# A rotary swap by one VectorE shuffle, and mask, scale and row maximum of attention scores in one VectorE operation per head and query tile

## The chip, the cores and the metric

The kernel runs on one core of a Trainium2 chip. The metric is the device time of one execution in microseconds (us), the median of several runs. The core's engines work side by side, each through an in-order queue of its own: TensorE (PE) multiplies matrices into PSUM, VectorE (DVE) and ScalarE (ACT) compute on PSUM and SBUF, GpSimd (POOL) computes on SBUF, and SyncE (SP) issues most transfers. They wait for one another by semaphores.

## The reference, cut to what matters

The input x is 4 x 512 x 1024 in fp32. It is layer-normalized; an attention with rotary embedding (16 heads of 64) and a gate (a linear layer with the signs of its weights, scaled by routed expert scales, then SiLU) are computed from it, and the result is x + attention * gate.

```python
def _rotate_every_two(x):
    r = jnp.stack((x[..., 1::2], x[..., ::2]), axis=-1)
    return r.reshape(x.shape)

def _apply_rotary(x, sin, cos):
    sin = jnp.repeat(sin[None, :, None, :], 2, axis=3)
    cos = jnp.repeat(cos[None, :, None, :], 2, axis=3)
    return x * cos + _rotate_every_two(x) * sin
...
q = jnp.concatenate([_apply_rotary(q[..., :ROT], sin, cos), q[..., ROT:]], axis=-1)
k = jnp.concatenate([_apply_rotary(k[..., :ROT], sin, cos), k[..., ROT:]], axis=-1)
...
logits = jnp.einsum('bhqd,bhkd->bhqk', q, k)
causal = jnp.tril(jnp.ones((s, s), dtype=bool))[None, None]
logits = jnp.where(causal, logits, MASK_VAL)
logits = logits / jnp.sqrt(jnp.float32(HEAD_DIM))
attn = jax.nn.softmax(logits, axis=-1)
out = jnp.einsum('bhqk,bhkd->bhqd', attn, v)
...
xn = _layernorm(x, axis=-1)
s = _L0_attn_ref(xn, L0_attn_Wq, L0_attn_Wk, L0_attn_Wv, L0_attn_Wo)
g = _silu(_L0_ffn_ref(xn, L0_ffn_weight, L0_ffn_bias, ...))
x = x + s * g
```

Two things of it matter here. The rotary embedding pairs each even column of a head with the odd column beside it: it needs, next to q and k themselves, a copy in which neighbours have changed places. And the scores are masked causally, scaled by 1/8 and put through a softmax over the keys.

## The kernel before

*Stages.* The work falls into an attention stage (to about 780 us of the profiled execution), a short stage in which the last attention units run beside the gate's first products, and an output stage of Strassen products for the gate and the output projection (from about 825 us). PE's instructions have an order written out by hand: the kernel's Python code emits them in the order in which PE runs them. DVE, ACT, POOL and SP are ordered by the scheduler, except where the code pins an instruction, and during the first 27 us for DVE and ACT.

*Attention.* For each of the 4 batches and each of 4 groups of head pairs, Q, K and (for two groups at once) V are projected by seven Strassen products each (`project_qk`, `project_v`). Between the matmuls of these projections, the attention of the group before is interleaved in pieces: a group has two units, each a pair of heads (two times 64 partitions). That makes 32 units. One unit goes through:

1. `rotary` (L313), once for Q and once for K, each a tile `c` of 128 partitions (2 heads x 64) by 512 positions. The host has reordered the columns of Wq and Wk so that the 32 even columns of a head come first and its 32 odd columns after them. The swapped copy `sw` is thus four block copies of 32 partitions (L319, L320 on ACT), with the factor 1/8 for Q. DVE multiplies `c` with the cosines (L321), POOL multiplies `sw` with the sines and adds (L322, L323).
2. `scores` (L508): for the query tiles 3, 2, 0, 1 (128 queries each, against 512, 384, 128 and 256 keys) two heads each, into PSUM. Tiles 3, 2 and 0 use the pool `ps_sc`; tile 1 uses two banks of the ring of four (`bank`), which the projections use too.
3. `softmax` (L533), first for tiles 1 and 3 and in a later piece for 2 and 0: DVE adds the mask to the diagonal 128 columns (L545), and takes the negated row maximum (L548), for both heads at once except in tile 1; ACT computes the exponential with that bias and sums it (L551, each followed by a read of its accumulator); DVE inverts the sum (L559), POOL multiplies (L561).
4. `transpose_blocks` (L569): DVE transposes blocks of 32 x 32 (L579), and sixteen transfers on SP's queue set them into place (L589).
5. `values` (L596): the products with V into one ring bank (L604), which ACT copies out (L613); then a transfer to DRAM.

The ring of four PSUM banks is what ties the engines together: a projection's product, the two score banks of tile 1, the p·V bank and the transposes of x all take their turn in it, and PE can start on a bank only when ACT or DVE has emptied it. In the projections, ACT copies out parts (L358, L387), DVE adds them (L352, L389) and forms the Strassen sums of the next weights (`form_w`, L288).

*Around it.* The next batch's x is normalized (L171 to L187), transposed by PE (L200) and copied from PSUM to `X`, on DVE where the test of L203 holds (13 copies, L204) and else on ACT (19 copies, L206). The router of a batch (`router`) uses `gw` and writes a transposed result `rT` (L671).

Of the kernel before, what the change touches and what calls it, by code (L numbers as in the profile page):

```python
# [9 lines left out]
F32 = mybir.dt.float32  # L10
F32R = mybir.dt.float32r
AF = mybir.ActivationFunctionType
ALU = mybir.AluOpType
AX = mybir.AxisListType
# [6 lines left out]
B, S, E = 4, 512, 1024  # L21
H, D = 16, 64
NE = 8
P = 128
NT = B * S
NC = E // P
NPAIR = H // 2
NGRP = NPAIR // 2
TPB = S // P
# [2 lines left out]
MASK_VAL = -1000000000.0  # L32
EPS = 1e-05
SCALE = 0.125

QCOL = [0, P, 3 * P, 6 * P]
OFF = [0, 128, 256, 224]


@with_exitstack
def attn_gated_ffn_kernel(
# [15 lines left out]
    nc = tc.nc  # L59
# [3 lines left out]
    cp = ctx.enter_context(tc.tile_pool(name="const", bufs=1))  # L63
    st = ctx.enter_context(tc.tile_pool(name="stats", bufs=4))
# [2 lines left out]

    ident = cp.tile([P, P], F32, name="ident")
    make_identity(nc, ident)
    mask = cp.tile([P, P], F32, name="mask")  # L70
    nc.gpsimd.memset(mask, 0.0)
    nc.gpsimd.affine_select(
        out=mask,
        in_=mask,
        compare_op=ALU.is_ge,
        fill=MASK_VAL,
        base=0,
# [6 lines left out]
    warm = cp.tile([P, 1], F32, name="warm")  # L84
    nc.scalar.activation(warm, eps, AF.Sqrt)

    gw = cp.tile([P, NC, 32], F32, name="gw")
    nc.gpsimd.memset(gw, 0.0)

# [5 lines left out]
    for sign, base in ((1, 0), (-1, 7)):  # L97
        nc.gpsimd.affine_select(
            out=high,
            in_=high,  # L100
# [29 lines left out]
    def left(*a, **k):  # L130
        return pctx.enter_context(tc.tile_pool(*a, **k))
# [6 lines left out]
    wp = left(name="w", bufs=3)  # L138
    tmp = left(name="tmp", bufs=2)
    tabs = left(name="tables", bufs=1)  # L140

    cos_sb = tabs.tile([P, S], F32, name="cos_sb")
    sin_sb = tabs.tile([P, S], F32, name="sin_sb")

    def bank(name):
        return ring.tile([P, S], F32, tag="r", name=name)

    def tp_bank(name):
        return bank(name).rearrange("p (t q) -> p t q", t=TPB)
# [44 lines left out]
    def transpose_x(b, t, g):  # L194
        if b not in X:
            X[b] = xp.tile([P, NC, S], F32, tag="X", name=f"X_{b}")
        tp = tp_bank(f"xtp_{b}_{t}_{g}")
        for j in range(4):
            c = 4 * g + j
            nc.tensor.transpose(tp[:, j, :], xin[b, t][:, c * P : (c + 1) * P], ident)  # L200
        dst = X[b][:, 4 * g : 4 * g + 4, t * P : (t + 1) * P]

        if (g == 0 and b > 0) or (g == 1 and (b, t) == (0, TPB - 1)):  # L203
            nc.vector.tensor_copy(dst, tp)  # L204
        else:
            nc.scalar.copy(dst, tp)  # L206
        if g == 1:

            queue = nc.scalar if (b, t) == (B - 1, TPB - 1) else nc.sync
            queue.dma_start(  # L210
                out=xn_d[b, t].rearrange("p (c q) -> p c q", c=NC),
                in_=X[b][:, :, t * P : (t + 1) * P],
            )
# [98 lines left out]

    def rotary(u, m, c):  # L313

        sc = SCALE if m == 0 else 1.0
        rot = qk.tile([P, S], F32, tag=f"rot{m}", name="rot%d_%d_%d_%d" % (m, *u))
        sw = tmp.tile([P, S], F32, tag="sw", name="sw%d_%d_%d_%d" % (m, *u))
        for r in range(0, P, 64):
            nc.scalar.activation(sw[r : r + 32, :], c[r + 32 : r + 64, :], AF.Copy, scale=sc)  # L319
            nc.scalar.activation(sw[r + 32 : r + 64, :], c[r : r + 32, :], AF.Copy, scale=sc)  # L320
        nc.vector.scalar_tensor_tensor(rot, c, sc, cos_sb, op0=ALU.mult, op1=ALU.mult)  # L321
        nc.gpsimd.tensor_tensor(sw, sw, sin_sb, op=ALU.mult)  # L322
        nc.gpsimd.tensor_tensor(rot, rot, sw, op=ALU.add)  # L323
        (Q, K)[m][u] = rot
# [177 lines left out]
    def probs(u, i):  # L502

        return PR[u][:, :, QCOL[i] : QCOL[i] + (i + 1) * P]
# [28 lines left out]
    def softmax(u, *tiles):  # L533
        un = "%d_%d_%d" % u
        for i in tiles:
            pt, ps = probs(u, i), SC[u, i]
            nmx = st.tile([P, 2], F32, tag="nmx", name=f"nmx_{un}_{i}")

            at_once = [(ps[h][:, None, :], slice(h, h + 1)) for h in range(2)]
            if i != 1:  # L540
                at_once = [(ps, slice(0, 2))]
                ps = [ps[:, h, :] for h in range(2)]
            for v, hs in at_once:
                diag = v[:, :, i * P : (i + 1) * P]
                nc.vector.tensor_tensor(  # L545
                    diag, diag, mask[:, None, :].to_broadcast((P, hs.stop - hs.start, P)), op=ALU.add
                )
                nc.vector.tensor_reduce(nmx[:, hs], v, AX.X, ALU.max, negate=True)  # L548
            ssum = st.tile([P, 2], F32, tag="ssum", name=f"ssum_{un}_{i}")
            for h in range(2):  # L550
                nc.scalar.activation(  # L551
                    pt[:, h, :],
                    ps[h],
                    AF.Exp,
                    bias=nmx[:, h : h + 1],
                    accum_out=ssum[:, h : h + 1],
                )
            rs = st.tile([P, 2], F32, tag="rs", name=f"rs_{un}_{i}")
            nc.vector.reciprocal(rs, ssum)  # L559
            for h in range(2):  # L560
                nc.gpsimd.tensor_scalar(  # L561
                    pt[:, h, :], pt[:, h, :], rs[:, h : h + 1], 1.0,
                    op0=ALU.mult, op1=ALU.mult,
                )
# [4 lines left out]
    def transpose_blocks(u, queues=(nc.sync,), ordered=False):  # L569
# [4 lines left out]
        for j in range(TPB):  # L574
            for i in range(j, TPB):
                src = probs(u, i)[:, :, j * P : (j + 1) * P]
                o = OFF[j] + 32 * (i - j)
                tc.keep_in_program_order(
# [17 lines left out]
    def values(u):  # L596
# [3 lines left out]
        for j in range(TPB):  # L600
            for h in range(2):
                r = h * D
                o = 320 * h + OFF[j]
                nc.tensor.matmul(  # L604
# [19 lines left out]
    def router(b, step):  # L624
        if step == 0:
            lg = bank(f"lg_{b}")[:, :P]
            for c in range(NC):
                for t in range(TPB):
                    nc.tensor.matmul(
                        lg[32 * t : 32 * t + 32, :],  # L630
                        lhsT=gw[:, c, :],
                        rhs=X[b][:, c, t * P : (t + 1) * P],
                        start=(c == 0),
                        stop=(c == NC - 1),
                    )
            R["lg"] = st.tile([P, P], F32, tag="r", name=f"lgs_{b}", bufs=1)
            nc.scalar.copy(R["lg"], lg)
        elif step == 1:
            lt = bank(f"lt_{b}")[:, :P]
            nc.tensor.transpose(lt, R["lg"], ident)  # L640
            ltg = lt.rearrange("p (t e) -> p t e", e=32)[:, :, :NE]
            nmx = st.tile([P, TPB], F32, tag="rmx", name=f"rmx_{b}")
            nc.vector.tensor_reduce(nmx, ltg, AX.X, ALU.max)
            ex = st.tile([P, TPB, 32], F32, tag="r", name=f"rex_{b}", bufs=1)
            exv = ex[:, :, :NE]
            nc.vector.tensor_tensor(
                exv, ltg, nmx[:, :, None].to_broadcast((P, TPB, NE)), op=ALU.subtract
            )
            nc.scalar.activation(exv, exv, AF.Exp)
            ssum = st.tile([P, TPB], F32, tag="rsum", name=f"rsum_{b}")  # L650
            nc.vector.tensor_reduce(ssum, exv, AX.X, ALU.add)
            rs = st.tile([P, TPB], F32, tag="rrs", name=f"rrs_{b}")
            nc.vector.reciprocal(rs, ssum)
            nc.vector.tensor_tensor(
                exv, exv, rs[:, :, None].to_broadcast((P, TPB, NE)), op=ALU.mult
            )

            hi = st.tile([P, TPB, NE], F32R, tag="rhi", name=f"rhi_{b}", bufs=1)
            nc.vector.tensor_copy(hi, exv)
            hi = hi.bitcast(F32)  # L660
            for n in (3, 2):
                nc.vector.tensor_tensor(
                    ex[:, :, n * NE : (n + 1) * NE], exv, hi, op=ALU.subtract
                )
            for n in (1, 0):
                nc.vector.tensor_copy(ex[:, :, n * NE : (n + 1) * NE], hi)
            R["ex"] = ex
        else:
            rt = bank(f"rt_{b}")[:, :P]
            nc.tensor.transpose(rt, R["ex"].rearrange("p t e -> p (t e)"), ident)  # L670
            rT = st.tile([P, P], F32, tag="rT", name=f"rT_{b}", bufs=1)  # L671
            nc.vector.tensor_copy(rT, rt)
            for t in range(TPB):
                nc.sync.dma_start(out=rt_d[b, t], in_=rT[32 * t : 32 * t + 32, :])
# [215 lines left out]
    for k, (b, g) in enumerate(groups):  # L890
# [38 lines left out]
        if k in (5, 9, 12, 14):  # L929
            n = {5: 0, 9: 2, 12: 4, 14: 6}[k]  # L930
# [121 lines left out]
    w, v = late  # L1052
# [318 lines left out]
def _rotary_tables():  # L1371
    f = np.float32
    inv = (f(1.0) / (f(10000.0) ** (np.arange(0, D, 2, dtype=f) / f(D)))).astype(f)
    ang = (np.arange(S, dtype=f)[None, :] * inv[:, None]).astype(f)
    return np.tile(np.cos(ang), (4, 1)).astype(f), np.tile(np.sin(ang), (4, 1)).astype(f)


# [49 lines left out]
```

## Time and profile before

| | |
|---|---|
| runs | 1107.7, 1110.0, 1110.54 us, median 1110.0 |
| span of the profiled execution | 1108.7 us |
| granted clock of PE, mean | 0.996 |
| ACT swaps, L319 and L320 | 256 times 628 ns, 160.7 us |
| DVE mask, L545 | 160 times, 57.0 us busy |
| DVE row maximum, L548 | 160 times, 105.2 us busy |
| ACT exponentials, L551 | 256 times, 132.9 us busy |
| POOL rotary products, L322 and L323 | 128 times, 175.9 us busy |

How to read the lines: a row of a group names the line of the kernel, the engine, the operation, the tiles (out<-in) and shapes, how often it ran, then busy time in us and the mean of one in ns, and last the idle time of that engine just before these instructions and who ended most of it. A row of the waits says which engine and line waited for which, in total us, how often, and the longest. A timeline row begins with the start and the length in us; what stands in brackets is the idle time before it. PE runs each fp32 matmul in two passes, so that "x16" stands for eight matmuls of the code. A row of stretches gives the bounds, the length, and the busy time of PE, the weight loads, DVE, ACT and POOL (with their number of instructions), then the granted clock, the share of the transfers and GB/s. The mean of one instruction contains the overlap with its neighbour; the busy time counts overlaps once.

### The profile page before, as it was taken

The numbers are of one execution on the slowest core, as the hardware profiler recorded it, in microseconds if no ns is written. First come the engines' busy times: TensorE is split into PE (matmuls) and PEld (weight loads), VectorE is DVE, ScalarE is ACT, GpSimd is POOL, SyncE is SP. The second block draws the span as 40 slices with busy tenths as digits, with TensorE's granted clock in tenths as the row PEclk, the third lists the DMA queues.
The fourth block names the chain that finished last, engine by engine and source line by source line (L and its number), as shares of the span: only waits on it lengthen the run. The fifth ranks groups of instructions, "written<-read, shape, count | busy, mean of one in ns | idle before, by whom it ended". The sixth has DMA issues, their size and how long they took to land. (4 is left out here: it accounts for less than half of the span.)

```text
span 1108.7 us, 15895 instructions
## 1 busy us (share of the span) xinstructions
PE 1087.4 (98%) x5176; PEld 790.2 (71%) x5176; DVE 870.4 (79%) x1740; ACT 461.3 (42%) x1072; POOL 518.9 (47%) x566
## 2 busy tenths in 40 slices
PE   9999999999999999999999999999999999999997
PEld 8887778777777877777788687777664545654663
DVE  7888888788988978888887887887776877567663
ACT  2452754453375445427544452655530223122220
POOL 0772645555264555526453562675552433432334
PEclk9999999999999999999999999999999999999999
DMA  9415566544556654455666445544664222431331
GB/s 323 135 69 147 149 184 189 160 137 119 166 155 187 190 154 135 121 163 158 184 183 219 140 148 142 153 125 122 179 193 171 90 93 102 148 119 54 136 114 57
DMA packets 86770, 163.88 MB, mean 148 GB/s; under 512 B 13472, under 2 KB 49056, under 8 KB 80672
## 3 DMA queue, kind: packets, MB, share of 16 engines
q1 hardware_dynamic: 80144, 152.25, 46.1%
q0 software_dynamic: 4832, 9.05, 2.4%
q10 hardware_dynamic: 1712, 1.57, 0.5%
q8 instruction: 41, 0.67, 0.3%
q14 instruction: 41, 0.34, 0.1%
HBM read 95.45 MB, written 25.43 MB: 109 GB/s over the span
## 5 line engine op out<-in xcount | busy, mean ns | idle before, releaser
L561 POOL TENSOR_SCALAR p<-p,rs 128x256 f32<-128x256 f32 (+3 forms) x256 | 183.7, 734 | 200.6 <-DVE rs L559 136.2
L551 ACT ACTIVATE p<-sc,nmx 128x256 f32<-128x256 f32 (+3 forms) x256 | 132.9, 529 | 104.8 <-DVE nmx L548 87.2
L338 PE MATMUL pj<-X,w 128*128 128x256 f32 x576 | 134.3, 382 | 1.7 <-ACT p L551 1.5
L338 PE MATMUL pj<-T,S 128*128 128x256 f32 x512 | 120.5, 385 | 8.5 <-ACT v L613 8.5
L579 DVE STREAM_TRANSPOSE y<-p 128x256 f32<-128x256 f32 x320 | 112.4, 409 | 18.3 <-POOL p L561 16.9
L322 POOL TENSOR_TENSOR sw<-sw,sin_sb 128x512 f32<-128x512 f32 x64 | 85.1, 1330 | 81.1 <-ACT sw L320 75.4
L338 PEld LDWEIGHTS pj<-X,w 128*128 128x128 f32 x576 | 108.1, 190 | 20.0 <-issue 2.9
L338 PEld LDWEIGHTS pj<-T,S 128*128 128x128 f32 x512 | 96.7, 192 | 24.8 <-ACT v L613 11.3
L319 ACT ACTIVATE sw<-c 32x512 f32<-32x512 f32 x128 | 80.3, 628 | 70.0 <-DVE c L352 68.2
L338 PE MATMUL pj<-T,w 128*128 128x256 f32 x448 | 106.6, 382 | 0.0
L548 DVE TENSOR_REDUCE nmx<-sc 128x1 f32<-128x256 f32 (+3 forms) x160 | 105.2, 683 | 1.3
L425 PE MATMUL pj<-w,X 128*128 128x256 f32 x416 | 94.6, 380 | 0.8 <-ACT p L551 0.5
L338 PEld LDWEIGHTS pj<-T,w 128*128 128x128 f32 x448 | 83.4, 190 | 15.5 <-issue 4.6
L323 POOL TENSOR_TENSOR rot<-rot,sw 128x512 f32<-128x512 f32 x64 | 90.8, 1419 | 5.0
L425 PEld LDWEIGHTS pj<-w,X 128*128 128x128 f32 x416 | 78.2, 190 | 12.7 <-ACT p L551 2.0
L545 DVE TENSOR_TENSOR sc<-sc,mask 128x256 f32<-128x256 f32 (+1 forms) x160 | 57.0, 371 | 35.3 <-PE sc L525 35.3
L320 ACT ACTIVATE sw<-c 32x512 f32<-32x512 f32 x128 | 80.4, 628 | 1.6
L425 PE MATMUL pj<-w,T 128*128 128x256 f32 x352 | 80.2, 381 | 0.0
L525 PE MATMUL sc<-rot,rot 64*128 64x128 f32 (+3 forms) x512 | 79.7, 443 | 0.3 <-DVE v L451 0.3
L604 PE MATMUL pv<-p,v 128*64 128x256 f32 (+3 forms) x512 | 76.0, 439 | 0.4 <-issue 0.4
L388 POOL TENSOR_TENSOR part<-part,part 128x256 f32<-128x256 f32 x32 | 24.7, 771 | 105.2 <-ACT part L387 102.0
L613 ACT COPY v<-pv 128x512 f32<-128x512 f32 x32 | 18.7, 585 | 131.5 <-PE pv L604 131.4
(177 smaller groups left out, 1956.9 us busy)
## 6 DMA issues: line engine op xcount, KB each, us to landing
p<-y SPq DMA_DIRECT2D x496, 80.0 KB, 2.1
w<-in_wqk SPq DMA_DIRECT2D x31, 1024.0 KB, 5.3
w<-in_wv SPq DMA_DIRECT2D x16, 1024.0 KB, 5.2
x<-in_x SPq DMA_DIRECT2D x16, 512.0 KB, 4.3
at_d<-v SPq DMA_DIRECT2D x32, 256.0 KB, 2.7
xp<-xn_d SPq DMA_DIRECT2D x16, 512.0 KB, 4.6
ap<-at_d SPq DMA_DIRECT2D x16, 512.0 KB, 5.1
xr<-in_x SPq DMA_DIRECT2D x32, 256.0 KB, 3.0
```

Source lines behind the costliest of these rows:

```text
L319: nc.scalar.activation(sw[r : r + 32, :], c[r + 32 : r + 64, :], AF.Copy, scale=sc)
L320: nc.scalar.activation(sw[r + 32 : r + 64, :], c[r : r + 32, :], AF.Copy, scale=sc)
L322: nc.gpsimd.tensor_tensor(sw, sw, sin_sb, op=ALU.mult)
L323: nc.gpsimd.tensor_tensor(rot, rot, sw, op=ALU.add)
L338: nc.tensor.matmul(ps, lhsT=wq[:, k, :], rhs=xq[:, k, :], start=(k == 0), stop=(k == 3))
L425: nc.tensor.matmul(ps[:, j, :], lhsT=xq[:, k, j * P : (j + 1) * P], rhs=wq[:, k, :], start=(k == 0), stop=(k == 3),)
L525: nc.tensor.matmul(head(i, h), lhsT=Q[u][r : r + D, i * P : (i + 1) * P], rhs=K[u][r : r + D, : (i + 1) * P], start=True, stop=True,)
L548: nc.vector.tensor_reduce(nmx[:, hs], v, AX.X, ALU.max, negate=True)
L551: nc.scalar.activation(pt[:, h, :], ps[h], AF.Exp, bias=nmx[:, h : h + 1], accum_out=ssum[:, h : h + 1],)
L561: nc.gpsimd.tensor_scalar(pt[:, h, :], pt[:, h, :], rs[:, h : h + 1], 1.0, op0=ALU.mult, op1=ALU.mult,)
L579: nc.vector.transpose(out[:, :, :, o : o + 32], src.rearrange("p h (b c) -> p h b c", b=4))
L604: nc.tensor.matmul(by_block[r : r + D, :, 32 * j :], lhsT=V[u][:, j, r : r + D], rhs=PT[u][:, :, o : o + 32 * (TPB - j)], start=(j == 0), ...
```

## The change

Rotary: the host leaves the columns of Wq and Wk in their order and lays the tables out for it, so that the swap is between neighbouring partitions. The four ACT copies become one `stream_shuffle` on DVE with the pattern n ^ 1 within each 32 partitions. The factor 1/8 leaves the rotary embedding.

Softmax: mask and maximum become one `tensor_tensor_reduce` for each head and tile over the tile's whole row: it adds the mask (now 512 columns wide, zero but for the last 128, and sliced so that the diagonal block falls onto these), multiplies by -1/8, writes the result back to PSUM and folds it with min from 3e38. That minimum is the negated row maximum. ACT's exponential gets the scale -1. In the built program each such operation is two DVE instructions, the second of which has the 128x1 result alone as its output.

Besides, `gw` and `rT` are placed in the pool of the tables, and twelve of the thirteen copies of transposed x that DVE made are made by ACT. PE's order of instructions is the same.

```diff
+FAR = 3e38
+NEIGHBOUR = [n ^ 1 for n in range(32)]
...
-    mask = cp.tile([P, P], F32, name="mask")
+    mask = cp.tile([P, S], F32, name="mask")
     nc.gpsimd.memset(mask, 0.0)
     nc.gpsimd.affine_select(
-        out=mask,
-        in_=mask,
+        out=mask[:, S - P :],
+        in_=mask[:, S - P :],
...
-    gw = cp.tile([P, NC, 32], F32, name="gw")
-    nc.gpsimd.memset(gw, 0.0)
...
+    gw = tabs.tile([P, NC, 32], F32, name="gw")
+    nc.gpsimd.memset(gw, 0.0)
...
-        if (g == 0 and b > 0) or (g == 1 and (b, t) == (0, TPB - 1)):
+        if g == 1 and (b, t) == (0, TPB - 1):
             nc.vector.tensor_copy(dst, tp)
         else:
             nc.scalar.copy(dst, tp)
...
-        sc = SCALE if m == 0 else 1.0
         rot = qk.tile([P, S], F32, tag=f"rot{m}", name="rot%d_%d_%d_%d" % (m, *u))
         sw = tmp.tile([P, S], F32, tag="sw", name="sw%d_%d_%d_%d" % (m, *u))
-        for r in range(0, P, 64):
-            nc.scalar.activation(sw[r : r + 32, :], c[r + 32 : r + 64, :], AF.Copy, scale=sc)
-            nc.scalar.activation(sw[r + 32 : r + 64, :], c[r : r + 32, :], AF.Copy, scale=sc)
-        nc.vector.scalar_tensor_tensor(rot, c, sc, cos_sb, op0=ALU.mult, op1=ALU.mult)
+        nc.vector.stream_shuffle(sw, c, NEIGHBOUR)
+        nc.vector.tensor_tensor(rot, c, cos_sb, op=ALU.mult)
         nc.gpsimd.tensor_tensor(sw, sw, sin_sb, op=ALU.mult)
         nc.gpsimd.tensor_tensor(rot, rot, sw, op=ALU.add)
...
-            at_once = [(ps[h][:, None, :], slice(h, h + 1)) for h in range(2)]
             if i != 1:
-                at_once = [(ps, slice(0, 2))]
                 ps = [ps[:, h, :] for h in range(2)]
-            for v, hs in at_once:
-                diag = v[:, :, i * P : (i + 1) * P]
-                nc.vector.tensor_tensor(
-                    diag, diag, mask[:, None, :].to_broadcast((P, hs.stop - hs.start, P)), op=ALU.add
-                )
-                nc.vector.tensor_reduce(nmx[:, hs], v, AX.X, ALU.max, negate=True)
+            for h in range(2):
+                nc.vector.tensor_tensor_reduce(
+                    out=ps[h],
+                    in0=ps[h],
+                    in1=mask[:, (TPB - 1 - i) * P :],
+                    scale=-SCALE,
+                    scalar=FAR,
+                    op0=ALU.add,
+                    op1=ALU.min,
+                    accum_out=nmx[:, h : h + 1],
+                )
...
                     AF.Exp,
                     bias=nmx[:, h : h + 1],
+                    scale=-1.0,
                     accum_out=ssum[:, h : h + 1],
...
-            rT = st.tile([P, P], F32, tag="rT", name=f"rT_{b}", bufs=1)
+            rT = tabs.tile([P, P], F32, tag="rT", name=f"rT_{b}", bufs=1)
...
-    return np.tile(np.cos(ang), (4, 1)).astype(f), np.tile(np.sin(ang), (4, 1)).astype(f)
+    ang = np.tile(np.repeat(ang, 2, axis=0), (2, 1))
+    return np.cos(ang).astype(f), np.sin(ang).astype(f)
...
-        w = w.reshape(E, H, D // 2, 2).transpose(0, 1, 3, 2).reshape(E, E)
```

## The prediction

> **What bounds the kernel now.** I read the page's busy shares first, then who TensorE (PE) waited for, then the instructions in order of time around its longest waits, and last the rows of the groups that the change touches.
>
> ```profile
> span 1108.7 us, 15895 instructions
> ...
> PE 1087.4 (98%) x5176; PEld 790.2 (71%) x5176; DVE 870.4 (79%) x1740; ACT 461.3 (42%) x1072; POOL 518.9 (47%) x566
> ```
> ```profile
> PE pj L338 <- ACT v L613: 8.5, 7, 2.3
> PE os L783 <- ACT p L551: 2.0, 1, 2.0
> ...
> PE pj L338 <- ACT p L551: 1.5, 2, 1.1
> ```
>
> PE is busy for 98% of the span, and its matmuls follow one another at a fixed pace (128x256 in 216 ns: sixteen take 3.5 us in the timeline). So neither VectorE (DVE, 79%) nor ScalarE (ACT, 42%) is worth its busy time; each is worth only what PE waits for it. That list is short. The largest entry is seven waits, 8.5 us in all, for the ACT copy that empties the PSUM bank of p·V (L613). The timelines of ACT and of PE at one of them:
>
> ```profile
> 714.83 0.63 ACT L319 ACTIVATE sw<-c 32x512 f32<-32x512 f32 x1 [5.62 <-DVE c L352]
> ...
> 719.32 0.62 ACT L320 ACTIVATE sw<-c 32x512 f32<-32x512 f32 x1
> 719.97 0.59 ACT L613 COPY v<-pv 128x512 f32<-128x512 f32 x1
> ```
> ```profile
> 713.43 2.37 PE L604 MATMUL pv<-p,v 128*64 128x512 f32 x16
> ...
> 720.61 3.72 PE L338 MATMUL pj<-T,S 128*128 128x256 f32 x16 [1.81 <-ACT v L613]
> ```
> ```profile
> 623.50 5.41 PE L338 MATMUL pj<-T,S 128*128 128x256 f32 x16 [2.34 <-ACT v L613]
> ```
>
> The p·V products end at 715.80. Their copy starts only at 719.97, because eight rotary swaps of 0.63 us stand ahead of it in ACT's queue, and the projection that takes the freed bank starts at 720.61. The last line shows what a longer wait brings: after 2.34 us without work the same sixteen matmuls take 5.41 us and not 3.72, since the granted clock is halved for 3.4 us; that is 1.7 us more. The 2.0 us wait for the exponentials at 802.6 is followed by another such stretch (the matmuls from 805.08 to 808.5 start every 0.43 us, then every 0.23).
>
> **The change, part by part.** The rows it is costed with:
>
> ```profile
> L545 DVE TENSOR_TENSOR sc<-sc,mask 128x256 f32<-128x256 f32 x96 | 39.6, 423 | 35.3 <-PE sc L525 35.3
> L545 DVE TENSOR_TENSOR sc<-sc,mask 128x128 f32<-128x128 f32 x64 | 18.7, 293 | 0.0
> ...
> L171 DVE BATCH_NORM_STATS2 bn<-x 128x6 f32<-128x512 f32 x32 | 20.5, 673 | 8.6 <-DMA x<-in_x 8.6
> ...
> L321 DVE SCALAR_TENSOR_TENSOR rot<-c,cos_sb 128x512 f32<-128x512 f32 x64 | 45.3, 734 | 0.2
> ...
> L559 DVE RECIPROCAL rs<-ssum 128x2 f32<-128x2 f32 x128 | 20.5, 160 | 25.3 <-ACT p L551 23.8
> ...
> L551 ACT ACTIVATION_READ_ACCUMULATOR p<-sc,nmx 128x1 f32 x256 | 51.9, 203 | 0.0
> ```
> ```profile
> 0.00:780.00 780.00, 766.88 (x4110) 608.38 (x4112) 649.12 (x1405) 376.75 (x911) 390.30 (x441) 1.00 0.55 159
> ```
>
> *ACT.* All 256 swap activations go: 80.3 + 80.4 = 160.7 us. Twelve of the thirteen transposed-x copies of L204 come over from DVE, 12 x 0.584 (the row of L206) = 7.0 us. In the changed program's ACT queue the copy of p·V stands behind a copy of a projection part or an exponential of the unit before, never behind a swap.
>
> *Softmax on DVE.* Mask and reduction leave: 57.0 + 105.2 = 162.2 us busy, 5.07 us for each of 32 units. In come 256 fused passes over 512, 384, 256 and 128 elements. No row shows them. The nearest is the mask add, which also reads PSUM and SBUF and writes PSUM: (423 - 293)/128 = 1.02 ns per element and 163 ns fixed, so 685, 555, 424 and 294 ns; 64 of each make 125.3 us, less some 0.08 us of overlap between neighbours (two reductions at 719.07 take 1.55 us together, 1.64 by their means), 256 x 0.08 = 20.5: 104.8 us. The program lists each pass as two instructions, the second writing the 128x1 accumulator. Between 0.08 net (the reciprocal, 160 ns less overlap, same engine) and 0.20 (ACT's accumulator read) I take 0.10, near the first: 25.6 us. 128 second heads wait for DVE's own first pass; a mask add followed by the reduction that waits for it loses that 0.08 us and 0.03 more: 128 x 0.11 = 14 us. Sum 144 us against 162: 18 us less. Bounds: 105 (the two extras hidden) to 105 + 51 + 14 = 170.
>
> *Rotary on DVE.* 64 shuffles of 128x512 come in. [...] The cosine product turns from 734 into some 685 ns (L389): -3 us. The twelve copies leave: 12 x 0.68 = -8 us.
>
> *DVE in sum:* -18 + 38 - 3 - 8 = +9 us, between -47 and +60. DVE goes to some 880 us, and of the first 780 us it holds 658 and not 649.
>
> [...]
>
> *Where PE feels it.* (1) The seven waits for L613 end: the copy can run at 715.8 to 716.4, PE asks at 718.8. -8.5 us, and -1.7 for the halved clock after 623.50. (2) The three waits for exponentials of the 128x256 tile (1.5 at L338, 0.5 at L425): the first maximum is ready after one pass and not after three masks and a reduction. At 497.37 that chain ends at 498.78; with one pass of 0.42 + 0.10 it ends near 497.9. 0.9 us earlier against waits of 0.4 to 1.1: -2.0. (3) The wait at 802.6: DVE begins this softmax at 796.40 and ACT's exponentials at 799.22, after a table load of 1.28 us; begun 0.9 us sooner, and with the last tile's chain of mask and reduction (0.41 + 0.43) replaced by passes that let the first exponential go after 0.4, the last of them ends some 1.5 us sooner: -1.5, and with 0.5 us of idling left no halved clock, -1.7. (4) The mask's memset is 128x512 and stands before the identity's select on GpSimd (POOL); 128x128 takes 0.20 us and 128x256 0.30, so 0.50. PE's first work waits for the identity, +0.3.
>
> (5) What the shuffles delay. In DVE's queue two of them stand between the sum of a projection and the next unit's fused passes, 1.2 us. Behind them stand the weight forms S of the next projection: formed from 722.64 to 727.31, they are first read at 733.42 and 735.2, so 7.8 us are to spare there. That cover hides 1.2 us; without it each of 32 units would cost PE up to 1.2 us, 38 us. POOL's rotary products wait for the shuffle in place of four activations (2.5 us), which is earlier. The moved router buffers (gw, rT) only change which pool holds them. For small new waits, in the first 65 us above all, where DVE runs almost without a gap, I add 2 us.
>
> Sum: -8.5 - 1.7 - 2.0 - 1.5 - 1.7 + 0.3 + 2 = -13.1. The profiled execution spans 1108.7 us, the three runs lie from 1107.7 to 1110.5 with a median of 1110.0, so it stands for them within 1.3 us. **1110.0 - 13.1 = 1097 us**; with none of the 2 us of new waits 1095, and with the wait of (3) gone whole 1094.
>
> **The rivals.** *The waits move, and nothing is left.* PE arrives 13 us earlier over the span at banks that DVE empties. For it: DVE is at 84% of the first 780 us, and its queue is in order. Against: in the whole span PE waits for DVE for 0.8 us (0.3, 0.3 and 0.2). If every removed wait came back as one for a DVE sum, 1110 + 0.3: 1110.
>
> [...]
>
> *It gains, but only in ACT's queue.* If the fused pass is later than mask and reduction, only (1) is left: 1110 - 10.2 + 2.3 = 1102.
>
> **How the numbers follow.** Forecast (near 1097) 0.52; only ACT's queue (1102) 0.16; the waits move (1110) 0.11; DVE bound, in part or whole (1114 to 1140), 0.21. About 0.3%, 3.3 us, is what this kernel's runs can tell from no change, so 1106.7 to 1113.3 counts as the same. The first two are faster: 0.68; same 0.11; slower 0.21. Range 1093 to 1122: the floor with every listed wait gone, less a little, up to the middle of the second rival; the forecast's own range is 1094 to 1102.
>
> **What would show it.** No wait of PE for L613; swaps gone from ACT and its busy time near 308 us; fused passes near 0.69 us for 512 elements, 64 shuffles near 0.68; DVE near 880 us; no halved clock in the middle. A fused pass above 0.9 us at 512 elements, a PE list headed by DVE sums, or PE busy below 97% would make it wrong.

## The result: slower by 0.34%, and the profile after

The changed kernel takes 1113.4 us (median of 8 runs, 1111.1 to 1114.4), the kernel before 1109.5 us (8 runs, 1107.7 to 1110.5): ratio 1.0034, 95% interval 1.0024 to 1.0044. The forecast was 1097. The page of the changed kernel, span and busy times, and then the head of the list of who TensorE (PE) waited for (us in total, times, longest):

```profile
span 1112.4 us, 15940 instructions
...
PE 1090.9 (98%) x5176; PEld 794.2 (71%) x5176; DVE 873.5 (79%) x2048; ACT 311.8 (28%) x828; POOL 523.4 (47%) x566
```
```profile
PE sc L525 <- DVE v L451: 3.1, 3, 1.9
PE pv L608 <- DMA at_d<-v: 2.8, 1, 2.8
PE pj L338 <- DVE part L352: 2.6, 2, 2.2
PE rt L674 <- DVE rex L670: 2.1, 1, 2.1
PE idle L804 <- POOL ident masks.py:199: 1.9, 1, 1.9
PE sc L525 <- DVE part L352: 1.8, 2, 1.4
PE os L787 <- ACT p L554: 0.9, 1, 0.9
```

Every wait that the change was meant to shorten is gone or smaller: no wait for ScalarE's (ACT's) copy of p·V at L613 (8.5 us before), none for an exponential at a projection (2.0), 0.9 for 2.0 at `os`. In their place stand waits for VectorE (DVE), 10.5 us over the whole list, where there were 0.8, and one of 2.8 for the transfers of the last unit. PE's idle time, span less busy, is 21.5 us after and 21.3 before. So the waits have moved, and their sum has not changed. The other 3.5 us are in PE's busy time, and nearly all of that is the clock. Windows of PE (start:end and length, busy, instructions, granted clock, DMA share, GB/s):

```profile
88.71:92.12 3.41, 1.82 (x8) 1.00 0.60 137
92.12:95.53 3.41, 3.41 (x10) 0.50 0.56 126
...
740.65:744.06 3.41, 1.25 (x8) 1.00 0.63 159
744.06:747.47 3.41, 3.41 (x10) 0.50 0.57 130
```

After the waits at 88.4 and 740.7 the clock is halved for 3.41 us, which costs 1.7 us each. The kernel before has two such stretches ahead of its end (624.4 and 805.3), this one four (92.1, 648.5, 744.1, 826.0): 2 x 1.7 = 3.4 us. The two profiled executions differ by 3.7 us: 0.2 of idling and 3.5 of busy time. How many stretches there are is not the same in every run: the eight runs of the changed kernel have mean clocks from 0.992 (1114.4 us, the profiled one) to 0.996 (1111.1 us).

Where the time is lost can be read off directly, because PE runs the same instructions in the same order in both kernels: compare the starts of one instruction. The changed kernel is 2.5 us late at 37.9, 4.1 us late at 90.3, level at 523.5 (the L613 waits have gone), 3.5 us early at 625.2, late again by 1.2 us at 742.8 and by 2.8 behind the halved stretch there. It wins this back where the exponentials kept PE waiting before, and is level at 817.9 (817.80 before). Then come the last unit's p·V products and the first products of the output stage, in the kernel before and in the changed one:

```profile
822.58 2.38 PE L604 MATMUL pv<-p,v 128*64 128x512 f32 x16 [0.36 <-issue]
824.88 3.70 PE L1240 MATMUL wo<-wo,ap 128*128 128x512 f32 x8
```
```profile
825.08 3.69 PE L608 MATMUL pv<-p,v 128*64 128x512 f32 x16 [2.77 <-DMA at_d<-v]
828.70 3.60 PE L1244 MATMUL wo<-wo,ap 128*128 128x512 f32 x7
```

This wait and the halved stretch behind it leave PE 3.8 us late, and little changes after that. The transfer that the profile names lands at 825.34, when PE has already started; it cannot be the one. The last of the sixteen transfers that set the transposed blocks into place (`p<-y`) lands at 824.67, 0.41 us ahead of PE's start. In the kernel before it landed at 822.17, again 0.41 us ahead, and PE was there only 0.36 us too early. The ten transposes before these transfers begin at 813.32 in place of 811.22: this chain stayed late where PE caught up. The softmax part alone (below) has this wait too, 2.4 us with a halved stretch behind it, so it does not need the rotary part. Most of what follows is about the time before, in which 8.5 us of waits went and nothing was gained.

What the new operations cost, from the groups of instructions kept apart by shape (busy us, mean ns of one, idle before):

```profile
L321 DVE TENSOR_TENSOR rot<-c,cos_sb 128x512 f32<-128x512 f32 x64 | 57.6, 900 | 0.0
L320 DVE STREAM_SHUFFLE sw<-c 128x512 f32<-128x512 f32 x64 | 47.4, 741 | 0.0
L542 DVE CUSTOM_DVE_ANT_0 sc<-sc,mask 128x512 f32<-128x512 f32 x64 | 46.8, 731 | 0.0
L542 DVE DVE_READ_ACCUMULATOR2_ANT nmx<- 128x1 f32 x256 | 36.0, 141 | 0.0
```

The fused pass and the shuffle cost about what was said (0.65 and 0.62 us from one start to the next; where a pass follows, the accumulator read starts together with it and adds nothing). Together the rows of L542 keep DVE busy for 129.6 us, where mask and maximum took 162.2. The cosine product does not cost what was said: forecast 0.685, before 0.734, now 0.900 us. It is the same product, without its factor. What is new is what runs beside it.

### One wait, followed back

The wait at 88.4 of the changed kernel, in the timelines of PE, DVE and GpSimd (POOL) (start, duration, and in brackets the idle time before and who ended it):

```profile
90.30 0.67 PE L525 MATMUL sc<-rot,rot 64*128 64x256 f32 x2 [1.86 <-DVE v L451]
```
```profile
78.29 0.15 DVE L563 RECIPROCAL rs<-ssum 128x2 f32<-128x2 f32 x1
82.69 1.75 DVE L583 STREAM_TRANSPOSE y<-p 128x256 f32<-128x256 f32 x5 [4.24 <-POOL p L565]
84.36 0.72 DVE L451 TENSOR_TENSOR v<-pj,part 128x256 f32<-128x256 f32 x2
85.00 1.73 DVE L583 STREAM_TRANSPOSE y<-p 128x256 f32<-128x256 f32 x5
86.65 0.65 DVE L291 TENSOR_TENSOR S<-w 128x512 f32<-128x512 f32 x1
...
89.40 0.75 DVE L451 TENSOR_TENSOR v<-pj,part 128x256 f32<-128x256 f32 x2
```
```profile
73.80 1.71 POOL L322 TENSOR_TENSOR sw<-sw,sin_sb 128x512 f32<-128x512 f32 x1
75.58 1.70 POOL L323 TENSOR_TENSOR rot<-rot,sw 128x512 f32<-128x512 f32 x1
77.27 2.11 POOL L565 TENSOR_SCALAR p<-p,rs 128x384 f32<-128x384 f32 x2
79.35 1.26 POOL L322 TENSOR_TENSOR sw<-sw,sin_sb 128x512 f32<-128x512 f32 x1
80.69 1.27 POOL L323 TENSOR_TENSOR rot<-rot,sw 128x512 f32<-128x512 f32 x1
81.94 0.72 POOL L565 TENSOR_SCALAR p<-p,rs 128x128 f32<-128x128 f32 x2
```

The same place in the kernel before (POOL, DVE and PE):

```profile
77.84 0.72 POOL L561 TENSOR_SCALAR p<-p,rs 128x128 f32<-128x128 f32 x2
78.52 1.27 POOL L322 TENSOR_TENSOR sw<-sw,sin_sb 128x512 f32<-128x512 f32 x1
```
```profile
78.59 2.08 DVE L579 STREAM_TRANSPOSE y<-p 128x256 f32<-128x256 f32 x6 [3.93 <-POOL p L561]
```
```profile
86.20 0.67 PE L525 MATMUL sc<-rot,rot 64*128 64x256 f32 x2 [0.30 <-DVE v L451]
```

Read the first group from the bottom. POOL scales the last probabilities at 81.94. Two rotations stand ahead of them in its queue; in the kernel before only one did, and these scalings ran at 77.84. DVE's transposes wait for them 4.24 us, at the head of an in-order queue. Behind the transposes and four weight forms stands the sum of L451 that empties PE's bank. PE names DVE; DVE had been waiting for POOL.

DVE waited for POOL in the kernel before as well, 3.93 us, and PE hardly noticed (0.30). What counts is the lateness against PE, whose score products just ahead start at 86.01 now and at 83.48 before, 2.53 us later. Scalings, transposes and the sum are each 4.1 us later, so 1.57 us late against PE, and PE's wait grew by 1.56.

Why POOL is late has two parts. Its sine product used to wait for four ScalarE copies; now it can start when the shuffle ends, and in POOL's queue, which the scheduler orders, the second rotation has come ahead of the scalings: it holds POOL for 2.59 us (79.35 to 81.94). And the first rotation runs at the same moment as DVE's own cosine products; its two operations take 3.41 us in place of 2.53. In the prologue a small operation of DVE ends only when one of POOL does (DVE and then POOL):

```profile
33.92 1.24 DVE L663 CAST rhi<-rex 128x32 fp32r<-128x32 f32 x1
```
```profile
33.43 1.70 POOL L323 TENSOR_TENSOR rot<-rot,sw 128x512 f32<-128x512 f32 x1
```

The cast of 128x32 took 0.18 us before; here it takes 1.24 and ends at 35.16, when POOL's addition ends (35.13). The subtraction after it (1.20 us, to 36.40; 0.19 before) and a copy (0.91, to 37.75; 0.18 before) end with POOL's next operations (36.35 and 37.71) in the same way, and PE waits 2.1 us for their result (`rt`, at 37.9). The three stalls, some 2.8 us, are more than this wait; without the collision it would not be there. Of the cosine products that stand singly in the timeline of the first 700 us, three met an idle POOL and took 0.68 us each; 53 overlapped POOL for over a quarter of their length and took 0.92 us in the mean, 2.13 at most. The sums of L352, with one input in PSUM, take 0.41 us in both cases.

### The profile page after: what moved, and what is told of

Read it like the earlier page. It is cut to its first block, busy times and chain, and to the rows that moved or that the text cites. A ratio compares the mean times of both kernels' runs of the same rounds, so it can differ in the third digit from the quotient of the medians.

```text
span 1112.4 us, 15940 instructions
## 1 busy us (share of the span) xinstructions
PE 1090.9 (98%) x5176; PEld 794.2 (71%) x5176; DVE 873.5 (79%) x2048; ACT 311.8 (28%) x828; POOL 523.4 (47%) x566
## 3 DMA queue, kind: packets, MB, share of 16 engines
q10 hardware_dynamic: 1712, 1.57, 0.5%
## 5 line engine op out<-in xcount | busy, mean ns | idle before, releaser
L565 POOL TENSOR_SCALAR p<-p,rs 128x256 f32<-128x256 f32 (+3 forms) x256 | 173.3, 691 | 278.9 <-DMA p<-y 87.2
L542 DVE CUSTOM_DVE_ANT_0 sc<-sc,mask 128x256 f32<-128x256 f32 (+3 forms) x256 | 120.7, 505 | 39.8 <-PE sc L525 39.0
L583 DVE STREAM_TRANSPOSE y<-p 128x256 f32<-128x256 f32 x320 | 111.2, 408 | 20.7 <-POOL p L565 20.6
L322 POOL TENSOR_TENSOR sw<-sw,sin_sb 128x512 f32<-128x512 f32 x64 | 98.1, 1533 | 56.6 <-DVE sw L320 52.6
L338 PEld LDWEIGHTS pj<-X,w 128*128 128x128 f32 x576 | 108.3, 190 | 21.3 <-DVE part L352 3.4
L338 PE MATMUL pj<-T,S 128*128 128x256 f32 x512 | 118.1, 379 | 0.0
L525 PE MATMUL sc<-rot,rot 64*128 64x128 f32 (+3 forms) x512 | 82.3, 445 | 5.3 <-DVE v L451 3.1
L425 PEld LDWEIGHTS pj<-w,T 128*128 128x128 f32 x352 | 67.1, 193 | 11.0 <-issue 2.0
L525 PEld LDWEIGHTS sc<-rot,rot 64*128 64x128 f32 x512 | 43.8, 186 | 36.8 <-issue 22.9
L608 PEld LDWEIGHTS pv<-p,v 128*64 128x64 f32 x512 | 34.7, 138 | 48.2 <-issue 38.6
L338 PE MATMUL pj<-X,S 128*128 128x256 f32 x256 | 62.1, 384 | 0.0
```

The lines of the kernel that those rows point to most:

```text
L338: nc.tensor.matmul(ps, lhsT=wq[:, k, :], rhs=xq[:, k, :], start=(k == 0), stop=(k == 3))
L425: nc.tensor.matmul(ps[:, j, :], lhsT=xq[:, k, j * P : (j + 1) * P], rhs=wq[:, k, :], start=(k == 0), stop=(k == 3),)
L525: nc.tensor.matmul(head(i, h), lhsT=Q[u][r : r + D, i * P : (i + 1) * P], rhs=K[u][r : r + D, : (i + 1) * P], start=True, stop=True,)
L542: nc.vector.tensor_tensor_reduce(out=ps[h], in0=ps[h], in1=mask[:, (TPB - 1 - i) * P :], scale=-SCALE, scalar=FAR, op0=ALU.add, op1=ALU.mi ...
L565: nc.gpsimd.tensor_scalar(pt[:, h, :], pt[:, h, :], rs[:, h : h + 1], 1.0, op0=ALU.mult, op1=ALU.mult,)
L583: nc.vector.transpose(out[:, :, :, o : o + 32], src.rearrange("p h (b c) -> p h b c", b=4))
```

## The experiments

Theories when they began: **A**, DVE's queue (shuffles ahead of sums); **B**, the fused pass; **C**, the collision of the two engines. **D**, POOL's queue (scalings behind rotations, transposes behind scalings, sums behind transposes), was formed from the second group. Each kernel was timed in 4 to 12 runs beside 8 to 23 of the kernel before; the ratio is to that, taken over all runs and not from the two medians. Three kernels leave out a part of the work: the rotary part alone leaves out the factor 1/8, the two named "no" the sine product and the swap. The last three columns are from the lists of waits of one execution each, us.

| kernel | median us | ratio (95%) | DVE waits for POOL's p | PE waits for DVE | for ACT |
|---|---|---|---|---|---|
| before | 1109.5 | | 16.9 | 0.8 | 12.7 |
| changed | 1113.4 | 1.0034 (1.0024-1.0044) | 20.6 | 10.5 | 1.1 |
| rotary part alone | 1126.1 | 1.0159 (1.0140-1.0178) | 25.4 | 14.9 | 7.3 |
| softmax part alone | 1105.1 | 0.9953 (0.9939-0.9967) | 8.5 | 0.5 | 9.1 |
| copies back | 1111.4 | 1.0016 (1.0007-1.0025) | 19.4 | 10.2 | 1.0 |
| cosine first | 1107.7 | 0.9996 (0.9984-1.0008) | 14.7 | 9.8 | 1.0 |
| no sine product | 1097.2 | 0.9889 (0.9876-0.9902) | 8.7 | 1.6 | 1.0 |
| no shuffle | 1125.2 | 1.0136 (1.0119-1.0153) | 45.7 | 15.6 | 1.4 |
| cosine first, copies back | 1110.7 | 0.9993 (0.9982-1.0005) | 12.0 | 9.7 | 1.0 |
| swap by DMA | 1108.5 | 0.9996 (0.9986-1.0005) | 7.2 | 6.9 | 3.2 |
| cosine on GpSimd | 1124.9 | 1.0129 (1.0113-1.0144) | 67.4 | 16.2 | 1.0 |
| sine on VectorE | 1101.6 | 0.9928 (0.9916-0.9941) | 2.0 | 3.5 | 1.0 |
| whole rotation on VectorE | 1109.5 | 0.9995 (0.9986-1.0004) | 0.6 | 4.6 | 9.3 |
| ScalarE's swaps, sine on VectorE | 1119.4 | 1.0080 (1.0066-1.0094) | 1.9 | 9.4 | 9.4 |

### The two halves

```diff
 # rotary part alone: the kernel before with
-        for r in range(0, P, 64):
-            nc.scalar.activation(sw[r : r + 32, :], c[r + 32 : r + 64, :], AF.Copy, scale=sc)
...
+        nc.vector.stream_shuffle(sw, c, NEIGHBOUR)
+        nc.vector.tensor_tensor(rot, c, cos_sb, op=ALU.mult)
```

> The kernel before with the rotary part of the change alone: shuffle and plain cosine product on VectorE, neighbouring columns, tables to match; the mask addition and the row maximum stay two operations per query tile. The factor 1/8 of the scores is left out. Theory A (the shuffles and the slower cosine products stand in VectorE's queue ahead of the sums that free PSUM banks for TensorE, and only the shorter softmax pays part of it back): all of A's cost and none of the softmax's gain, so slower than the changed kernel's 1113.4 us, 1116 to 1122, with VectorE above 900 us busy and more than 12 us of TensorE waits for VectorE. Theory B (the fused pass itself costs, because it comes head by head and both passes wait for the last score tile): the rotary part alone is then the good half, 1100 to 1107, with few waits for the sums of L352.

1126.1 us, slower by 16.7: A's direction, and beyond its range. PE's waits for DVE are 14.9 us and DVE is busy for 910.8 us.

The other half is the changed kernel with the four copies, the old form of the cosine product (its factor now 1), the old column order and the transposed-x copies on VectorE put back.

> The changed kernel with the old rotary: four ScalarE copies per unit and matrix, columns in halves, old tables; the fused pass stays, and so do the moves of the transposed-x copies to ScalarE. Theory A: VectorE loses 64 shuffles (0.62 us from start to start) and the contention of its cosine products, so the waits for L352 and for v L451 shrink to under 4 us in all; 1103 to 1108 us, faster than both, though some waits for ScalarE's L613 come back. Theory B: the fused pass keeps its cost and ScalarE's queue is as full as it was, so 1113 to 1118, slower than before.

1105.1 us, faster than both. That expectation is wrong about its kernel in one point: the 12 copies of transposed x were on VectorE in it, as before. Its waits:

```profile
PE pj L341 <- ACT v L620: 8.0, 7, 2.4
PE pv L611 <- DMA at_d<-v: 2.4, 1, 2.4
```

No DVE row stands among the large ones, and the bank copy (L613 before, L620 here) is back with 8.0 of its 8.5 us. B falls: the fused pass is the good half. The rotary half removes ScalarE's waits at L613 and brings more at DVE.

### Copies, and the order of the pair

```diff
 # copies back
-        if g == 1 and (b, t) == (0, TPB - 1):
+        if (g == 0 and b > 0) or (g == 1 and (b, t) == (0, TPB - 1)):
 # cosine first
-        nc.vector.stream_shuffle(sw, c, NEIGHBOUR)
         nc.vector.tensor_tensor(rot, c, cos_sb, op=ALU.mult)
+        nc.vector.stream_shuffle(sw, c, NEIGHBOUR)
```

> The changed kernel with the 12 copies of transposed x back on VectorE. Theory A (lateness in VectorE's queue decides): about 12 x 0.69 = 8 us more in that queue, spread over three batches, of which some lands ahead of sums that TensorE waits for: 1114 to 1118 us. If VectorE's load does not decide: within 1 us of 1113.4.

1111.4 us: a miss for both lines. There are twelve more copies in DVE's queue (8 us), and the time is 1.9 us less; DVE's busy time, 873.0 us, did not rise; shorter cosine products, 860 ns in the mean, account for 2.6 of the 8 us. A, as the mere length of DVE's queue, is not borne out. Why it is a little faster was not followed up.

> The changed kernel with the cosine product ahead of the shuffle in VectorE's queue: the same two operations in the other order, so GpSimd's sine product no longer starts while the cosine product runs. Theory C (the two products running at once stretch VectorE's, 900 ns in the mean where 0.69 was forecast, and this makes the sums late): the cosine product falls below 750 ns in the mean, and the time to 1107 to 1111. Theory A without C (the 1.3 us of the pair, in whatever order, is what delays the sums): within 1.5 us of 1113.4, since the sums behind the pair start at the same time.

1107.7 us, where C put it, but not for C's reason: the cosine product still takes 844 ns in the mean, not under 750, and PE's waits for DVE are 9.8 us in place of 10.5. Its profiled execution has two halved stretches in place of four. The same wait of 1.86 us as at 88.4 is there, and its windows read:

```profile
89.19:92.60 3.41, 1.83 (x8) 1.00 0.60 137
92.60:96.01 3.41, 3.41 (x18) 1.00 0.55 126
```

Busy time 1.83 us against 1.82, and no halving. So part of this gain is where a wait falls and not how long it is. The runs say so too: seven at a granted clock of 0.997 took 1107.2 to 1108.5 us, three at 0.992 or 0.993 took 1111.8 to 1112.1, and one at 0.994 lies between (1109.1).

> The cosine product ahead of the shuffle and the 12 transposed-x copies back on VectorE. If the two gains (5.7 and 1.9 us against the changed kernel's median) are apart: 1105 to 1107. If both come from the same half-clock stretches: 1107 to 1109.

Neither: the twelve runs fall in two groups, 1106.6 to 1107.3 (clock 0.996 or 0.997, five runs) and 1110.6 to 1111.1 (0.992 to 0.994, seven), and the median of 1110.7 tells only which was more frequent. Differences of 4 us in this kernel can be the clock alone.

### What runs beside the cosine product

```diff
 # no sine product
-        nc.gpsimd.tensor_tensor(sw, sw, sin_sb, op=ALU.mult)
 # no shuffle
-        nc.vector.stream_shuffle(sw, c, NEIGHBOUR)
-        nc.gpsimd.tensor_tensor(sw, sw, sin_sb, op=ALU.mult)
+        nc.gpsimd.tensor_tensor(sw, c, sin_sb, op=ALU.mult)
```

> The changed kernel with GpSimd's sine product left out (64 operations of 1.5 us; the shuffled matrix is added to the rotated one unmultiplied). The shuffle and the cosine product stand where they stood in VectorE's queue; what goes is the operation that runs beside the cosine product. Theory C (the two engines slow each other): the cosine product falls to 0.68 to 0.72 us in the mean, VectorE loses some 12 us, and the time falls to 1104 to 1109. Theory A without C (the place in the queue alone decides): the pair still takes 1.3 us or more, 1110 to 1114.

> The changed kernel with the shuffle left out: GpSimd multiplies the unswapped matrix by the sine table, so its product starts beside the cosine product from the first nanosecond. VectorE loses 64 x 0.62 = 40 us of its queue and keeps the contention. Theory A: the waits of TensorE for the sums of L352 and for v L451 fall under 3 us, 1100 to 1106. Theory C (contention, not the shuffle's own time): the cosine product stays at 0.85 us or more and the gain is small, 1108 to 1112.

1097.2 and 1125.2 us. The first is faster than C's range, and yet its cosine product takes 882 ns (now it meets POOL's addition): C gave the direction, its row is wrong. So the stretch of DVE's cosine product is not what this kernel saved. The second takes 64 shuffles (47.4 us) away from DVE and is 11.9 us slower than the changed kernel: the times of A and C both miss. Its cosine product takes 1443 ns in the mean, since POOL's product starts beside it every time, and that alone returns 33 of the 47 us to DVE. So this kernel has a worse collision and a later queue at once, and does not tell them apart. DVE's waits for POOL's scaled probabilities, without the sine product and then without the shuffle (us in total, times, longest):

```profile
DVE y L582 <- POOL p L564: 8.7, 11, 2.8
```
```profile
DVE y L582 <- POOL p L564: 45.7, 14, 5.4
```

This column of the table goes, roughly, with the time among the kernels in which ScalarE holds up PE little; the cosine-first pair and the swap by DMA do not fit it closely. It is how D was formed: what counts is when POOL gets to the scalings.

> The changed kernel with the swap done by two DMAs of 64 rows each, issued in ScalarE's queue (even rows from odd rows and odd from even), so that neither VectorE nor ScalarE computes it. Theory A: VectorE's queue is as free as in the kernel with the softmax alone (about 830 us) and ScalarE's nearly as free as in the changed kernel, so neither L613's copies nor the sums come late: 1098 to 1104, faster than either. Against it: each swap then lands some 2 us after its issue (the dispatch's own landing times on this page's DMA rows are 2 us and more), 128 more DMAs of 128 KB compete with the weight loads, and scores whose rotary result comes late would show as TensorE waits for GpSimd's L323: 1108 to 1115.

1108.5 us, the pessimistic line. DVE is free of the shuffles (842.0 us busy) and the cosine product is down to 704 ns, but POOL waits 104.4 us for the swapped rows (landing 2.9 us after the issue, in the median), and ScalarE, which issues them, starts three of its copies of p·V late, by 24.1 us in all by the profile.

### GpSimd's queue, made longer and shorter

```diff
 # cosine on GpSimd
-        nc.vector.tensor_tensor(rot, c, cos_sb, op=ALU.mult)
+        nc.gpsimd.tensor_tensor(rot, c, cos_sb, op=ALU.mult)
 # sine on VectorE
-        nc.gpsimd.tensor_tensor(sw, sw, sin_sb, op=ALU.mult)
+        nc.vector.tensor_tensor(sw, sw, sin_sb, op=ALU.mult)
```

> The changed kernel with the cosine product on GpSimd: VectorE keeps the shuffle alone, GpSimd does both products and their sum, one after the other, some 3.8 us per rotation in place of 2.6. No cosine product is left for GpSimd to collide with, VectorE loses some 57 us, GpSimd gains 64 x 1.27 = 81 us. Theory C (collision of the two engines is the whole cost): 1099 to 1106. Theory D (the collision counts because it keeps GpSimd's queue long, and the scalings of the probabilities of L565 stand behind the rotations in that queue; VectorE's transposes wait for them and its sums behind the transposes): the longer rotations make the scalings later still, VectorE's wait for p L565 grows above 30 us, 1115 to 1130.

> The changed kernel with the sine product on VectorE: shuffle, cosine and sine product there, the addition alone on GpSimd. VectorE gains 64 x 0.60 = 38 us and loses the collision with GpSimd's sine product, GpSimd loses 98 us. Theory A (VectorE's queue decides by its length): 1120 to 1135. Theory D (GpSimd's queue decides): the scalings come as early as in the run without the sine product (1097), and VectorE pays some of it back: 1099 to 1108, faster than the kernel before.

1124.9 and 1101.6 us: D twice. Between these two the sign goes with POOL's load (594.0 and 428.2 us busy) and not with DVE's, which is 828.2 us busy in the slower kernel and 898.8 in the faster. In the first no cosine product is left on DVE to collide, and C put it at 1099 to 1106: the collision of these two products is not the whole cost. In the second the cosine product still takes 886 ns, against 900 in the changed kernel: the 11.8 us are not gained by a shorter cosine product. At the place of the wait shown above, with the cosine product on POOL (DVE and then PE):

```profile
83.63 2.08 DVE L583 STREAM_TRANSPOSE y<-p 128x256 f32<-128x256 f32 x6 [7.94 <-POOL p L565]
```
```profile
91.24 1.19 PE L525 MATMUL sc<-rot,rot 64*128 64x256 f32 x2 [3.74 <-DVE v L451]
```

and with the sine product on DVE (POOL and then DVE):

```profile
72.94 2.26 POOL L323 TENSOR_TENSOR rot<-rot,sw 128x512 f32<-128x512 f32 x1
75.19 1.15 POOL L565 TENSOR_SCALAR p<-p,rs 128x128 f32<-128x128 f32 x2
81.08 1.65 POOL L323 TENSOR_TENSOR rot<-rot,sw 128x512 f32<-128x512 f32 x1 [4.74 <-DVE sw L322]
```
```profile
76.37 1.75 DVE L583 STREAM_TRANSPOSE y<-p 128x256 f32<-128x256 f32 x5 [0.62 <-POOL p L565]
...
84.64 0.75 DVE L451 TENSOR_TENSOR v<-pj,part 128x256 f32<-128x256 f32 x2
```

The scalings run at 75.19 in place of 81.94, the transposes 6.3 us sooner, the sum at 84.64 in place of 89.40, while PE itself is 2.9 us earlier; it has no wait there. This kernel computes all of the reference and is faster than both: 1101.6 us, 0.7% below the kernel before. What is left are 3.0 us for L352, a wait of 4.0 for the last unit's transfers and two halved stretches, one of them of double length.

### How far that goes

```diff
 # whole rotation on VectorE: the sine product there, and
-        nc.gpsimd.tensor_tensor(rot, rot, sw, op=ALU.add)
+        nc.vector.tensor_tensor(rot, rot, sw, op=ALU.add)
 # ScalarE's swaps: the softmax part alone, and
-        nc.gpsimd.tensor_tensor(sw, sw, sin_sb, op=ALU.mult)
+        nc.vector.tensor_tensor(sw, sw, sin_sb, op=ALU.mult)
```

> The changed kernel with the whole rotation on VectorE: shuffle, both products and their sum. Against the run with the sine product alone moved (1101.6 us), VectorE gains 64 x 0.60 = 38 us and its cosine product falls from 886 to 0.68 us (-13), so some 924 us busy; GpSimd falls to 337. Theory D alone (only GpSimd's queue decides): as fast or faster, 1097 to 1102. Theory A beside it (VectorE's queue takes over once it is long enough): its transposes no longer wait for L565, but its sums come late for their own queue's length, TensorE's waits for VectorE grow from 3.5 to 10 us or more: 1106 to 1116.

1109.5 us, the second line. Little collides any more (701 ns for the cosine product). But PE's new waits are of another kind than that line named:

```profile
PE pj L425 <- ACT p L554: 5.2, 4, 1.4
PE os L787 <- ACT p L554: 3.2, 1, 3.2
PE sc L525 <- DVE v L451: 3.0, 1, 3.0
```

The largest are exponentials, which wait for row maxima. That DVE's own length now makes these late is the reading; which of its operations do was not tried.

> The kernel with the old swaps on ScalarE and the fused softmax (1105.1 us; its transposed-x copies are on VectorE), with the sine product moved from GpSimd to VectorE. Its VectorE wait for p L565 is 8.5 us already, so by theory D there is little left to gain in GpSimd's queue, and the ScalarE waits of 9.1 us stay: 1102 to 1106. If GpSimd's length costs in other ways too, the gain is as in the changed kernel (11.8 us): 1093 to 1097.

1119.4 us: both lines miss. Who DVE waited for:

```profile
DVE sw L325 <- ACT sw L323: 44.2, 50, 2.5
```

The sine product on POOL used to wait for the swaps at no cost to DVE; on DVE the wait stands in the queue of all sums. An operation was moved, and its wait with it: the same mistake as in the prediction, made again at another place.

## Why the prediction was wrong

**What held.** PE's seven waits for L613 went, 8.5 us, as step (1) said, and so did the three of step (2), 2.0. Step (3) gave 1.1 of its 1.5, and no halved clock follows it there. Step (4) is 0.4 for 0.3. ACT is 311.8 us for 308, the fused pass 731 ns for 0.69. No run shows what the 38 us for the shuffles in DVE's sum stand on; the 64 take 0.62 us each from one start to the next, 40 us. DVE is 873.5 us for 880, which is in part luck: softmax fell by 32.6 us and not by 18, because most of the accumulator reads, put at 25.6 us, are hidden, and the cosine product rose by 12.3 us where 3 less were forecast.

**Where the sum broke.** At the term "small new waits", +2, and at the clock. The new waits are 9.7 us more for DVE and 2.8 for the last unit, 12.5, somewhat more than the 11.6 that steps (1) to (3) took away. And the two halved stretches, put at -3.4, came to +3.4: the old two are gone and four others came, each behind a new wait.

**The step that failed is (5).** It looked for what the two shuffles delay in DVE's queue, found the weight forms with 7.8 us to spare, and stopped. Its +2 for all new waits measured 9.7 us at DVE, with three halved stretches of 1.7 behind them: 14.8, about all that (1) to (3) gained. In DVE's own queue it left out the transposes and the sums of L352 behind them, which cost 2.15 us at 742.8. Of POOL it said that its products wait for the shuffle in place of four activations, "which is earlier", and priced that at nothing. Earlier was the larger cost. It puts the sine product beside DVE's operations, which then took longer (the cast at the router 1.24 us for 0.18, with 2.1 us of PE's waits behind it; cosine products of 900 ns and not 685), and ahead of the scalings that DVE's transposes wait for. Moving that product off POOL is worth 11.8 us (1113.4 to 1101.6), leaving it out 16.2, and adding another to POOL costs 11.5. That the kernel without POOL's sine product takes 1097 us, the forecast, is chance.

**Step (3) stopped one wait too early.** It priced what PE gains at the exponentials, which came (1.1 us and the halved stretch). But the last unit's scalings, transposes and transfers are not sooner for it, and PE waits for them instead, 2.8 us and a halved stretch. The softmax part alone shows the same.

**The rivals.** "The waits move, and nothing is left", 1110 at a chance of 0.11, is what happened, with the clock on top; the engine it named was right and the evidence against it, 0.8 us of waits for DVE today, was a measure of the old order. DVE as the bound, to which the chance of 0.21 and the range's upper end of 1122 belong, did not happen. No run shows the slow fused pass that it needs: the pass takes 731 ns for 512 elements and 286 for 128, 1.16 ns per element. DVE is hardly busier than before (873.5 us against 870.4), and the kernel in which it is busier by 28 us is the faster.

**Left open.** How the changed kernel's loss divides between the collision and the order in POOL's queue. The wait at the router needs the collision; at 88.4 the second rotation's 2.59 us is more than the 1.57 by which the scalings are late, so the order alone would suffice there. For the other waits it was not worked out, and the direct test, scalings pinned ahead of the second rotation, was not run. At 742.8 the wait of 2.15 us for L352 is DVE's own queue, two shuffles and two cosine products of 2.9 us ahead of ten transposes; it stays with the sine product moved (2.20 at 728.3).

## What to carry to other kernels

Ask of a change not only what it delays but what it lets start sooner, in whose queue that stands and beside what it then runs. An engine's share of busy time says nothing of this: POOL, busy for 47%, held up PE through operations that stood behind its rotations. Follow a wait back past the engine that the profile names, to the queue in which that engine itself was waiting. And when a wait is removed, look for the next thing that the engine will then reach too early.

## What the runs showed of the hardware

In eight of this case's profiles the halved clock (0.50) came, ahead of the kernel's end, in stretches of 3.41 us or, at five places, twice that. In the changed kernel the four stretches begin 163, 28 and 24 times 3.413 us apart, in the kernel before the two begin 53 times that apart, and in five experiments the distances are such multiples as well: 16, 190 and 24 (cosine first, copies back), 180 and 24 (swap by DMA), 58, 58, 79 and 25 (cosine on GpSimd), 24 (sine on VectorE), 18 (ScalarE's swaps, sine on VectorE). The whole rotation on VectorE has one stretch, of double length.

Cut into windows of 3.413 us at these places, these profiles show, from 3 us to 1100 us: every window in which PE idled for 2.01 us or more was followed by a halved one, and none with less than 1.44 was, unless it was itself halved. Between them it went either way: 1.44 and 1.59 were followed by one in the changed kernel and 1.68 was not; 1.89 and 1.95 were (cosine first, copies back), 1.57 was not (whole rotation on VectorE), nor was the 1.58 of the cosine-first kernel above. What decides between 1.44 and 2.01 us no run here shows.
